# Two attention layers on one core: layer 0's output projection turned round to x1 transposed, by seven block products

## Chip, core and metric

The kernel runs on one core of a Trainium2 chip, in f32 throughout. The metric is device time in microseconds: the median of three runs of the kernel before is 2338.96 us (2338.3 to 2339.53). A profile of one further execution is used for every duration below.

## What is computed

The input x has 8 images of 32 x 32 = 1024 tokens and 256 channels. Layer 0 is attention with four heads, each as wide as all 256 channels, with an output projection, a bias and a residual. Layer 1 is attention with one head whose queries and keys have 32 channels; its values are scaled by gamma and added to its input.

```python
# layer 0
qkv = jnp.einsum('bnc,cd->bnd', xf, W_qkv)              # then split by head into q, k, v
atten = jnp.einsum('bihd,bjhd->bijh', q, k) * scale
atten = jax.nn.softmax(atten, axis=2)
res = jnp.einsum('bijh,bjhd->bihd', atten, v)
res = jnp.einsum('bnd,dc->bnc', res, W_out) + b_out + xf
# layer 1, on res
f, g, h = x@Wf + bf, x@Wg + bg, x@Wh + bh
y = gamma * (jax.nn.softmax(g f^T) @ h) + x
```

## The kernel before, in words

**Folded weights.** For each head, W_q W_k^T and W_v W_out are multiplied once (`fold_weights`, L293), so a head has only a query projection (wqk, C x C), scores against x itself, products of the exponentials with x itself, and an output projection (wvo, C x C). The exponentials are taken without subtracting a maximum; a flag made at the end from the inverse sums (`judge`, L997) chooses whether a general version is run afterwards.

**Seven products.** Query projection, scores and products are 2 x 2 block multiplications in the manner of Strassen and Winograd: seven block products in place of eight. `seven` (L234) returns three tasks. Task one makes products 1 (bank x), 6 (bank y) and 5 (bank z); ScalarE copies x to e, VectorE adds u = y + e. Task two adds product 2 to x and 7 to y; ScalarE copies x out, VectorE makes v = y + e and z + v. Task three adds 4 to y and 3 to z; VectorE adds y + e and z + u. The operands need four sums a side (`sum_a`, `sum_b`, L204 and L214), made by VectorE.

**Order of the work.** A step is a pair (unit, block): a unit is one head of layer 0 of one image (`Layer0`) or layer 1 of one image (`Layer1`), a block is 512 of the 1024 tokens. The units run image by image; layer 1 of image b-1 is put between heads 1 and 2 of image b, and that of image 6 after all heads of image 7. Layer 1 of image 7 (`final`) comes after the loop. PE, VectorE and ScalarE run in exactly the order in which the program issues their instructions (`manual_schedule`, L870); DMA queues on SP and the Pool engine are ordered by the framework. Within a step `put` (L922) gives every task a place between -2 and 11, and the tasks are issued in order of place. In a layer 0 step the score tasks have the places 0, 2, 4, 6, 8 and 10 (two times three tasks of `seven`). Around them lie, of the step before (`one`), the sums over its exponentials (`sums`, L559) with the sums over keys, and tasks one and two of its products; of the step before that (`two`), task three of its products, the inverse of its sums and its projection.

**Sums over keys.** For each block VectorE adds the sums that the products have made anyway: m (L585), then rs (L590, L591). Pool adds over partitions (`partition_all_reduce`, L593, 128 x 512) into rb; SP writes one row of rb to DRAM (L597) and reads it back as columns st (L600); VectorE inverts st (`invert`, L606).

**Projection.** `project` (L629) makes, per block, two tasks of four matmuls: y (128 channels x 128 tokens) is the stationary operand, wvo (128 x 256) the moving one. Rows of tokens come out in one bank po of the pool psm. VectorE multiplies by the inverse sum and adds to the rows of x1 (L648), which `residual` (L425) has filled with x + b_out.

**Layouts.** The scores need x transposed (xT), the products need x by rows. `load_x` loads rows; `turn_rows` (L357) turns rows into xT by DMAs of 32 x 32 squares and transposes on VectorE, a head before they are wanted; layer 1 needs x1 transposed, made in the same way through the fg tile as scratch, and by PE transposes for the last image (L986). `queries_apart` (L687) makes layer 1's f and g: PE, ScalarE into a tile with tag m0 (L698), then 16 SP DMAs (L718, L719), at the places 1.5 to 1.9 of the step before layer 1.

**Buffers.** The tags in L866 to L869 give the number of buffers: rows 4, xT 2, m0, ss, rs and rb 1 each; ps has six PSUM banks and psm two. m and fg2 share m0.

Of the kernel before, what the change touches and what calls it, by code (L numbers as in the profile page):

```python
# [10 lines left out]
F32 = mybir.dt.float32  # L11
# [9 lines left out]
def kernel(  # L21
# [14 lines left out]
):  # L36

# [111 lines left out]
    bout_sb = const.tile([P, C], F32, tag="bout", name="bout_sb")  # L149
    bfg_sb = const.tile([P, 1], F32, tag="bfg", name="bfg_sb")  # L150
# [7 lines left out]
    def load_rest():  # L158
        with nc.allow_non_contiguous_dma(reason="small bias vectors, loaded once"):
            nc.sync.dma_start(bout_sb, b_out.partition_broadcast(P))  # L160
# [20 lines left out]
    wblocks = {}  # L181
# [52 lines left out]
    def seven(name, width, parts, matmuls, outs, tags, copy, after=None):  # L234
# [7 lines left out]
        def bank(k):  # L242
            banks[k] = tile_of("ps", [P, NB], f"ps{k}_{name}")[:, :width]
# [22 lines left out]
        def one():  # L266
            for k, number in (("x", 1), ("y", 6), ("z", 5)):
                bank(k)
                product(k, number, True)
# [21 lines left out]
    NARROW = dict(e="eh", u="uh", v="w")  # L291

    def fold_weights(h):  # L293
# [20 lines left out]
        def multiply(i, what):  # L314
# [13 lines left out]
            if i == 0:  # L328
# [4 lines left out]
                wblocks[h] = b_operands(blocks, sums)  # L333

# [22 lines left out]
    def turn_rows(b, src, dst, layer, scratch=None):  # L357

# [5 lines left out]
        def end():  # L364
            if b not in dst:
                dst[b] = tile_of("xT", [P, CC, N], f"x{layer}T_{b}")
            return dst[b]

        def flat(t):
            return t.rearrange("p u n -> p (u n)").rearrange("p (s q) -> p s q", q=P)  # L370

        def move(a, c=None):
            to, rows_v = flat(end() if scratch is None else scratch()), flat(src[b])
            if c is not None:
                to, rows_v = to[:, ts(c, NT), :], rows_v[:, c::CC, :]
            for q in range(P // Q):
                nc.sync.dma_start(to[ts(q, Q), :, ts(a, Q)], rows_v[ts(a, Q), :, ts(q, Q)])

        def piece(k, c):
            to = end()[:, c, ts(k, NB)]  # L380
            if scratch is None:
                nc.vector.transpose(to, to)
            else:
                squares = scratch()[:, k, :].rearrange("p (t c q) -> p t c q", c=CC, q=P)
                nc.vector.transpose(to.rearrange("p (t q) -> p t q", q=P), squares[:, :, c, :])
# [39 lines left out]
    def residual(b):  # L425


        def piece(i):
            if i == 0:
                rows1[b] = tile_of("rows", [P, NT, C], f"x1_{b}")  # L430
# [702 lines left out]
```

## Time and profile before

| | |
|---|---|
| Median of three runs | 2338.96 us |
| The profiled execution's own time | 2338.61 us |
| Its span, first to last instruction | 2336.7 us |
| Granted TensorE clock | 0.999 |
| PE busy | 2326.9 us in 10394 matmul records |
| VectorE busy | 1481.7 us in 2398 instructions |
| ScalarE busy | 522.5 us in 875 instructions |
| Pool busy | 211.5 us in 79 instructions |
| DMA, mean | 18 GB/s |

The profile is one execution as the hardware profiler took it. A group's row gives line, engine, operation, the tiles written and read, the shapes and the count, then the busy time with the mean of one in ns, then the idle time of the engine just before, with what ended it. A timeline row gives start, duration, engine, line, operation and count. An engine's idle time costs only where it is on the chain that ends last. An f32 matmul shows as two records, and the ends of matmul records are modelled, so starts are the better measure.

### The profile page before, as it was taken

The numbers are of one execution on the slowest core, as the hardware profiler recorded it, in microseconds if no ns is written. First come the engines' busy times: TensorE is split into PE (matmuls) and PEld (weight loads), VectorE is DVE, ScalarE is ACT, GpSimd is POOL, SyncE is SP. The second block draws the span as 40 slices with busy tenths as digits, with TensorE's granted clock in tenths as the row PEclk, the third lists the DMA queues.
The fourth block names the chain that finished last, engine by engine and source line by source line (L and its number), as shares of the span: only waits on it lengthen the run. The fifth ranks groups of instructions, "written<-read, shape, count | busy, mean of one in ns | idle before, by whom it ended". The sixth has DMA issues, their size and how long they took to land.

```text
span 2336.7 us, 26026 instructions
## 1 busy us (share of the span) xinstructions
PE 2326.9 (100%) x10394; PEld 1918.8 (82%) x10394; DVE 1481.7 (63%) x2398; ACT 522.5 (22%) x875; POOL 211.5 (9%) x79
## 2 busy tenths in 40 slices
PE   9999999999999999999999999999999999999999
PEld 7888888788878888788887888878888788888877
DVE  6667775377754767557774577645776457766635
ACT  2222222222221222212222122221222222222222
POOL 0111111011110111101111011110011101101110
PEclk9999999999999999999999999999999999999999
DMA  4000010100101001110011000110001100000100
GB/s 138 1 1 1 1 37 14 34 1 11 27 17 32 1 19 21 19 29 1 19 26 18 24 1 19 30 18 19 1 19 30 19 19 1 1 1 1 30 7 31
DMA packets 170257, 42.94 MB, mean 18 GB/s; under 512 B 158160, under 2 KB 163024, under 8 KB 170128
## 3 DMA queue, kind: packets, MB, share of 16 engines
q1 hardware_dynamic: 170128, 41.20, 8.0%
q8 instruction: 84, 1.38, 0.3%
q14 instruction: 45, 0.37, 0.1%
HBM read 13.37 MB, written 8.52 MB: 9 GB/s over the span
## 4 chain that ended last, share of the span: by engine, by line
PE 99%; DVE 1%; DMA 0%; issue 0%; ACT 0%
PE psy_y L247 14%; PE psy L247 14%; PE psx L247 9%; PE pa_l L834 9%; PE po L637 9%; PE psx_y L247 9%; PE psz_y L247 9%; PE psz L247 9%; PE psy_q L247 4%; PE psx_q L247 2%; PE psz_q L247 2%; PE pr_v_l L466 2%; PE ps_l L746 1%; PE pm_fg L703 1%; PE pwqk L318 0%; PE pwvo L318 0%
## 5 line engine op out<-in xcount | busy, mean ns | idle before, releaser
L593 POOL PARTITION_ALL_REDUCE rb<-rs x64 | 206.9, 3233 | 2046.6 <-DVE rs L591 2019.8
L247 PE MATMUL psx<-q,x0T 128*128 128x256 f32 x1024 | 263.6, 380 | 0.0
L247 PE MATMUL psy<-qs,xs 128*128 128x256 f32 x1024 | 263.0, 379 | 0.0
L247 PE MATMUL psz<-q,xs 128*128 128x256 f32 x1024 | 262.8, 379 | 0.0
L541 ACT ACTIVATE p<-p 128x1024 f32<-128x1024 f32 x128 | 135.3, 1057 | 554.8 <-DVE p L264 554.8
L247 PE MATMUL psy_y<-s,xt 128*128 128x256 f32 x1024 | 242.4, 380 | 0.1
L637 PE MATMUL po<-wvo,y 128*128 128x256 f32 x1024 | 241.9, 379 | 0.0
L247 PE MATMUL psx_y<-p,x 128*128 128x256 f32 x1024 | 241.9, 379 | 0.0
L834 PE MATMUL pa_l<-v_l,s_l 128*128 128x257 f32 x1024 | 232.1, 381 | 0.4 <-DVE v_l L729 0.4
L247 PEld LDWEIGHTS psx<-q,x0T 128*128 128x128 f32 x1024 | 194.0, 190 | 45.2 <-issue 21.0
L637 PEld LDWEIGHTS po<-wvo,y 128*128 128x128 f32 x1024 | 194.6, 190 | 39.5 <-issue 14.8
L834 PEld LDWEIGHTS pa_l<-v_l,s_l 128*128 128x128 f32 x1024 | 193.8, 190 | 36.6 <-issue 10.5
L247 PEld LDWEIGHTS psx_y<-p,x 128*128 128x128 f32 x1024 | 194.7, 190 | 34.0 <-issue 8.6
L247 PEld LDWEIGHTS psy_y<-s,xt 128*128 128x128 f32 x1024 | 191.9, 190 | 30.6 <-issue 2.4
L247 PEld LDWEIGHTS psy<-qs,xs 128*128 128x128 f32 x1024 | 194.5, 190 | 27.0 <-DVE qs L512 0.4
L247 PEld LDWEIGHTS psz<-q,xs 128*128 128x128 f32 x1024 | 194.7, 190 | 26.3
L264 DVE TENSOR_TENSOR u<-psy,e 128x512 f32<-128x512 f32 x128 | 88.4, 691 | 144.3 <-ACT e L270 73.4
L276 ACT ACTIVATE p<-psx 128x512 f32<-128x512 f32 x128 | 76.4, 597 | 413.7 <-PE psx L247 413.6
L264 DVE TENSOR_TENSOR v<-psy,e 128x512 f32<-128x512 f32 x128 | 87.8, 686 | 124.5 <-PE psy L247 124.5
L247 PE MATMUL psy<-qs,x0T 128*128 128x256 f32 x512 | 131.6, 380 | 0.7 <-DVE v L264 0.7
L648 DVE SCALAR_TENSOR_TENSOR x<-po,inverse,x 128x256 f32<-128x256 f32 x256 | 111.9, 478 | 31.3 <-PE po L637 22.4
L270 ACT COPY e<-psx 128x512 f32<-128x512 f32 x128 | 73.8, 576 | 257.8 <-PE psx L247 257.8
(120 smaller groups left out, 2839.8 us busy)
## 6 DMA issues: line engine op xcount, KB each, us to landing
out_dram<-x SPq DMA_DIRECT2D x15, 512.0 KB, 2.6
x<-in_x_dram SPq DMA_DIRECT2D x14, 512.0 KB, 4.6
x0T<-x SPq DMA_DIRECT2D x224, 32.0 KB, 1.9
fg<-x SPq DMA_DIRECT2D x112, 64.0 KB, 2.1
fg<-fg SPq DMA_DIRECT2D x56, 64.0 KB, 2.0
w<-in_L_conv_W_qkv_dram SPq DMA_DIRECT2D x4, 512.0 KB, 7.3
x<-in_x_dram SPq DMA_DIRECT2D x4, 256.0 KB, 4.8
w<-in_L_conv_W_qkv_dram SPq DMA_DIRECT2D x4, 256.0 KB, 6.4
```

The costliest lines, as they stand in the source:

```text
L247: nc.tensor.matmul(banks[k][:, ts(i, w)], lhsT=lhsT, rhs=rhs, start=first and n == 0, stop=True, skip_group_check=True,)
L264: nc.vector.tensor_tensor(dst, shaped(banks[k]), shaped(other), ALU.add)
L270: nc.scalar.copy(scratch("e"), banks["x"])
L276: copy(outs["11"](), shaped(banks["x"]))
L466: nc.tensor.matmul(pm[:, ts(j, C)], lhsT=src()[:, c, ts(2 * t2 + j, P)], rhs=w()[:, c, :], start=(c == 0), stop=(c == CC - 1),)
L541: exp(both, both)
L593: nc.gpsimd.partition_all_reduce(t, r.rearrange("p e i -> p (e i)"), P, bass_isa.ReduceOp.add)
L637: nc.tensor.matmul(pm[:, ts(j, C)], lhsT=self.y[blk][:, c, ts(2 * t2 + j, P)], rhs=folded[self.h][1][:, c, :], start=(c == 0), stop=(c == ...
L648: nc.vector.scalar_tensor_tensor(acc, pm[:, ts(j, C)], inverse[:, n : n + 1], acc, ALU.mult, ALU.add)
L703: nc.tensor.matmul(pm[ts(k, half)], lhsT=w[:, c, :], rhs=x1T_of[b][:, c, ts(k, NB)], start=(c == 0), stop=(c == CC - 1),)
L746: nc.tensor.matmul(pm, lhsT=self.f[ts(r, CK), ts(j0 + r, P)], rhs=self.g[ts(r, CK), ts(blk, NB)], start=True, stop=True,)
L834: nc.tensor.matmul(pm[:, : C + 1], lhsT=p[:, j, ts(ti, P)], rhs=v[:, j, : C + 1], start=(j == 0), stop=(j == NT - 1),)
```

## The change

It turns the projection round. wvo is now the stationary operand, cut into four 128 x 128 blocks with their four sums (`oblocks`), and y the moving one, cut into two halves of 256 tokens a channel half, with four sums a block. `project` becomes a `seven` of three tasks with one matmul per product; its banks y and z share one bank of psm, x takes a bank of ps. The result o comes out transposed, channels by tokens, in a tile with tag m0. It is multiplied by the inverse sums spread over all partitions (rb) and added to x1T by an accumulating DMA that Pool issues. To have the inverse along the free axis, `invert` writes the inverted columns to a row in DRAM and reads it back to all partitions, two more DMAs on SP; in the last step `invert_all` inverts the all-reduced sums directly.

So x1 exists transposed first. `residual` fills x1T from xT on ScalarE with the bias by channel. Layer 1 reads x1T without a turn; its rows are made by `turn_back` with 32 DMAs an image, for the final additions. The last image's PE transposes go, and its fg projection moves behind the loop.

The sums over keys become three additions of 128 x 512, then one of 128 x 256; the product's sums s2 and s4 share a tile, and s3 overwrites the block a21. The query sums are made by block instead of by head. The next image's rows are loaded at head 1 instead of head 2, and the turns follow a step or two earlier than before; rows has 3 buffers, xT has 3. Head 3's weights are loaded into an xT buffer. Places change accordingly.

```diff
-    def seven(name, width, parts, matmuls, outs, tags, copy, after=None):
+    def seven(name, width, parts, matmuls, outs, tags, copy, after=None, two_banks=False):
...
         def bank(k):
-            banks[k] = tile_of("ps", [P, NB], f"ps{k}_{name}")[:, :width]
+            if not two_banks:
+                banks[k] = tile_of("ps", [P, NB], f"ps{k}_{name}")[:, :width]
+            elif k == "z":
+                banks[k] = banks["y z"][:, width : 2 * width]
+            else:
+                t = tile_of("psm", [P, NB], f"ps{k}_{name}")
+                banks["y z"], banks[k] = t, t[:, :width]
...
-                product(k, number, True)
+                product(k, number, k != "z" or not two_banks)
...
+            else:
+                t4 = const.tile([P, 4, P], F32, tag=f"wo{h}", name=f"wo{h}")
+                sums = [t4[:, k, :] for k in range(4)]
+                blocks = [t[:, c, ts(e, P)] for e in range(CC) for c in range(CC)]
+                run(sum_a(sums, *blocks))
+                oblocks[h] = a_operands(blocks, sums)
...
+            if c == 0:
+                x1T_of[b] = tile_of("xT", [P, CC, N], f"x1T_{b}")
+            nc.scalar.activation(
+                x1T_of[b][:, c, :], xT_of[b][:, c, :], AF.Identity, bias=boutT_sb[:, c : c + 1]
             )
...
+                    t = tile_of("qs", [P, 3, HB], f"qs_{self.name}_{blk}")
...
-                sums = [t[:, 1], s2, s3, t[:, 0]]
+                sums = [t[:, 1], t[:, 0], blocks[2], t[:, 0]]
...
+            def add(k):
+                t = made["t"]
+                if k == 1:
+                    made["r"] = tile_of("rs", [P, 2, HB], f"rs_{n}")
+                r = made["r"]
+                tt(r, t[:, :, 0, :] if k == 1 else r, t[:, :, k, :], ALU.add)
...
         def invert(self, blk):
...
+            inv = inverse[:, n : n + HT]
+            nc.vector.reciprocal(inv, self.r[blk])
+            if blk in self.rb:
+                return
+            line = tile_of("line", [1, NB], f"inv_{self.name}_{blk}")
+            with nc.allow_non_contiguous_dma(reason="columns turn into a row"):
+                nc.sync.dma_start(line.rearrange("o (t p) -> p (o t)", p=P), inv)
+            self.rb[blk] = t = tile_of("rb", [P, NB], f"invb_{self.name}_{blk}")
+            nc.sync.dma_start(t, line[0].partition_broadcast(P))
+
+        def invert_all(self, blk):
+
+            self.rb[blk] = t = tile_of("rs", [P, NB], f"invb_{self.name}_{blk}")
+            nc.vector.reciprocal(t, self.total[blk])
...
         def project(self, blk):
...
+                if i == 0:
+                    y = self.y[blk]
+                    t = tile_of("yt", [P, 3, HB], f"yt_{n}")
+                    blocks = [y[:, c, ts(e, HB)] for c in range(CC) for e in range(2)]
+                    sums = [blocks[1]] + [t[:, k] for k in range(3)]
+                    made["l"] = sum_b(sums, *blocks)
+                    made["b"] = b_operands(blocks, sums)
+                made["l"][i]()
+
+            def out(c, e):
+                if "o" not in made:
+                    made["o"] = tile_of("m0", [P, CC, NB], f"o_{n}")
+                return made["o"][:, c, ts(e, HB)].unsqueeze(1)
+
+            def add():
+                o = made["o"]
+                nc.vector.tensor_tensor(
+                    o, o, self.rb[blk].unsqueeze(1).broadcast_to([P, CC, NB]), ALU.mult
+                )
+                nc.gpsimd.dma_start(
+                    x1T_of[self.b][:, :, ts(blk, NB)], o, accum_op=ALU.add
+                )
...
+                lambda number: [(0, oblocks[self.h][number], made["b"][number])],
...
+            put([partial(u.invert, k)], 1.9)
+            ysums, tasks, add = u.project(k)
+            put(ysums, *((1.6, 1.7, 1.8, 3.2) if l0 else (2.6, 2.7, 2.8, 3.1) if blk == 0 else
+                         (1.1, 1.2, 1.3, 2.1)))
+            put(tasks, *((3, 5.5, 7) if l0 else (5.2, 6, 7.2) if blk == 0 else
+                         (3, 5, 7) if nxt else (2.1, 3, 4.5)))
+            put(add, 8.6 if nxt else 5)
...
-            put(sums[:2] + sums[3:], *((2.2, 3.2, 4.2) if l0 else (0.8, 2.2, 4.5)))
-            put(sums[2:3], 5.2 if l0 else 5.5)
-            put(keys, *((6.2, 8.2) if l0 else (7.6, 9.6)))
+            put(sums, *((0.9, 2.2, 4.2, 5.6) if l0 else (0.8, 2.2, 3.5, 5.5)))
+            put(keys, *((6.3, 6.6, 7.6, 8.7) if l0 else (6.3, 7.6, 8.3, 8.7)))
...
+        if l0 and blk == 0:
+            put(a.query_sums(1), 1.3, 2.3, 3.3, 4.3)
...
-        if l0 and a.h == 2 and blk == 0 and a.b + 1 < B:
+        if l0 and a.h == 1 and blk == 0 and a.b + 1 < B:
             load_x(a.b + 1)
...
+                moves, turned1 = turn_back(a.b - 1)
+                put(moves, *range(1, 9))
...
+            put(turned1, 0.6, 2.9, 4.2, 5.1)
         if nxt is None:
-            put(transpose_rows(B - 1, rows1, x1T_of, 1), 2.5, 4.5, 8.1, 8.2)
-            put(final.queries(), 2.4, 6.5, 9)
+            fg = final.queries()
+            moves, turned1 = turn_back(B - 1)
+            put(moves, *[9.1 + 0.1 * k for k in range(8)])
...
-    run(own[:1], s0[:1], prod[:1], p0[:1], s0[1:], prod[1:2], p0[1:2])
-    weave((prod[2:] + own[1:], 0, 1), (s1, 0.3, 0.7), (p1[:2], 0.55, 0.95), (p0[2:], 0.1, 0.9))
+    run(own[:1], prod[:1], fg, s0[:1], p0[:1], prod[1:2], s0[1:], p0[1:2])
+    weave((prod[2:] + own[1:], 0, 1), (s1, 0.3, 0.7), (p1[:2], 0.55, 0.95), (p0[2:], 0.1, 0.9), (turned1, 0.3, 1))
```

## The prediction

> **What bounds the kernel now.** First the page: busy shares and the chain that ended last.
>
> ```profile
> PE 2326.9 (100%) x10394; PEld 1918.8 (82%) x10394; DVE 1481.7 (63%) x2398; ACT 522.5 (22%) x875; POOL 211.5 (9%) x79
> PE 99%; DVE 1%; DMA 0%; issue 0%; ACT 0%
> ```
>
> TensorE is the bound: 2326.9 of 2336.7 us busy, 99% of the chain. A matmul less is time less unless PE starts to wait. Then PE's timeline, for what one matmul costs:
>
> ```profile
> 493.81 1.89 PE L637 MATMUL po<-wvo,y 128*128 128x256 f32 x8
> 495.54 1.03 PE L247 MATMUL psy<-qs,x0T 128*128 128x256 f32 x4
> ```
>
> Start to start, 8 records take 1.73 us. A 128x256 f32 matmul leaves two records (1024 records / 64 blocks = 16 for the 8 matmuls of L637's loops), so one costs **0.432 us**; the row mean of 380 ns counts overlap twice. Then the groups kept apart by shape, for VectorE and Pool:
>
> ```profile
> L593 POOL PARTITION_ALL_REDUCE rb<-rs x64 | 206.9, 3233 | 2046.6 <-DVE rs L591 2019.8 <-DVE y L264 26.8
> L648 DVE SCALAR_TENSOR_TENSOR x<-po,inverse,x 128x256 f32<-128x256 f32 x256 | 111.9, 478 | 31.3 <-PE po L637 22.4
> L580 DVE TENSOR_TENSOR ss<-p 128x1024 f32<-128x1024 f32 x64 | 77.7, 1214 | 0.0
> L585 DVE TENSOR_TENSOR m<-ss 128x1024 f32<-128x1024 f32 x64 | 77.8, 1215 | 0.8 <-DMA fg<-fg 0.7
> L590 DVE TENSOR_TENSOR rs<-m 128x512 f32<-128x512 f32 x64 | 43.5, 680 | 0.0
> L591 DVE TENSOR_TENSOR rs<-rs 128x256 f32<-128x256 f32 x64 | 27.2, 425 | 2.2
> L264 DVE TENSOR_TENSOR y<-psz_y,v_y 128x256 f32<-128x256 f32 x64 | 27.1, 424 | 2.2
> L382 DVE STREAM_TRANSPOSE x0T<-x0T 128x512 f32<-128x512 f32 x28 | 19.6, 701 | 0.0
> ```
>
> The row of m names a DMA as releaser. SP's and VectorE's timelines at that place (image 3, head 1, block 1):
>
> ```profile
> 942.51 0.59 SPq L719 DMA_DIRECT2D fg<-fg  x1
> 944.62 1.22 DVE L585 TENSOR_TENSOR m<-ss 128x1024 f32<-128x1024 f32 x1 [0.19 <-DMA fg<-fg]
> ```
>
> m and layer 1's fg2 (L698) share the one m0 buffer; m waits until the last of the 16 fg moves has landed. Then the windows view of a plain step, head 3's block 0 of image 1 (PE, PEld, DVE, ACT, POOL busy, in that order):
>
> ```profile
> 486.05:513.67 27.62, 27.62 (x129) 24.26 (x128) 22.72 (x37) 6.04 (x10) 4.94 (x2) 1.00 0.01 1
> ```
>
> VectorE is busy 82% of this step and PE has no gap. Last, PE near the end:
>
> ```profile
> 2306.34 3.92 PE L834 MATMUL pa_l<-v_l,s_l 128*128 128x257 f32 x17 [0.39 <-DVE v_l L729]
> ```
>
> At the tail VectorE already sets PE's pace.
>
> **What the skill says.** (1) "VectorE: DVE Perf Modes", The TRN2 errata: an f32 tensor_tensor takes (N+151)/0.96 ns: 424, 691, 1224 for 256, 512, 1024; the rows agree (425, 680, 1214), so halved width doesn't halve the price. (2) "PSUM — Partial Sum Buffer", PSUM bank collisions: two engines on one bank must be ordered, whatever the columns. Before, y and z have banks of their own, so the trace doesn't show it; with both in one, a VectorE read of y also waits for z's matmul. (3) "DMA: Bandwidth & Descriptors", Latency and other measured facts, and Anatomy of one DMA: a Pool-issued DMA costs about 1 us of emission, then about 2.0 us + bytes/436e3; an estimate for 512 KB is 1 + 3.2 us. No Pool DMA is in this trace.
>
> **The change, part by part**, against the profiled execution (2338.61 us: span 2336.7 + 1.9 around it; the runs' median is 2338.96).
>
> *Projection on PE.* 8 matmuls become 7, same shape: 64 x 0.432 = **-27.6 us**. Image 7's 8 transposes by PE go (px 0.49 + 0.43 + 0.87, start to start): **-1.8**. Both are on the path.
>
> *VectorE.* Per block: project was 4 x 0.478 = 1.91; it becomes 4 sums at 0.425, 5 adds at 0.424 and a 128x1024 multiply at 1.21, or 5.03. Keys: 1.215+0.680+0.425 = 2.32 becomes 3 x 0.680 + 0.425 = 2.47. Query sums: 2 x 0.685 becomes 4 x 0.425. Together +3.6 x 64 = +230; the residual's 21 us go to ScalarE (16 x 1.06). VectorE ends near 1,690 us, 73%: room on average, so what counts is order. I laid out one step by hand, block 0 of a head, from the start of its first score task, each instruction after its inputs (about 0.2 us from PE to VectorE, 0.06 back, as the timelines show). Third product task 2.6 to 6.05; score task two to 7.77; then the projection's first task needs t2 at 8.20. VectorE: last y add 6.25, one query sum, ysums 6.9, 7.3, 7.7: t2 ends 8.15. The reciprocal follows at 8.1, v at 8.2 to 8.9; score task three needs v at 9.07. So it fits with 0.05 to 0.15 us to spare. 25 such steps (both predecessors layer 0); bound 0 to 0.5 each, I take 0.04: **+1.0**. In block 1 the next queries' task gives 2.6 us more cover: nothing, and 0.4 each if backlog ate it. The same layout holds the other edits of a step: sum one moves ahead of the third product task into the idle before the y adds; sum four overwrites s2 and so waits for product y6, read by PE at 14.2, when VectorE arrives at 17.8; s3 in place of a21 waits for nothing younger. The value sums (block 1 of head 0) and turns keep 2 to 3 us of idle ahead of the product's tasks. 0 for all of these; half a microsecond a step if that idle is gone.
>
> *PSUM banks.* The projection's x takes one of the six ps banks from its first task to its second, beside three of the score and three of the product. The product's y and z need banks at 12.5 and 14.3; the score's x is free at 7.8, the last product's two at 5 and 6.7. No wait, so 0; at most 0.3 a step if a later bank is drawn (not in the sum). psm needs one bank a block instead of two.
>
> *Sums to columns and back.* The last key add moves to 8.7, behind the multiply and its Pool DMA. By the layout it ends 1.2 us before the step's end; DMA emission 1, all-reduce 3.23, then line and st as now (3.3 us from all-reduce to landing): st lands 6.0 us into the next step, needed at 8.1. Cost 0, cover 2.1 us; past it each us stops VectorE's queue, with v behind it, and PE. The new row and broadcast (SP, two DMAs, some 5 us) end by 14; the multiply comes at 23. Hidden.
>
> *fg moves against o.* The new o tile takes m0's single buffer. In the step of queries_apart (7 times) the clock from the score task's start (923.28 in image 3) is: pm_fg ends 8.0, fg moves landed 21.3 (944.6 above); invert now puts two more DMAs on SP, up to 1.2 later. The projection's second task runs 17.9 to 18.8 on PE, and its copy and add into o want m0 at 18.7, not at 21.3 as m did. ScalarE and VectorE stop there; the third task wants that bank's read at 21.4, and gets it at 21.3 + 0.5 to 22.5 + 0.5. Bound 0 to 2.5 per image, I take 1.2: 7 x 1.2 = **+8.4**.
>
> *Layer 1, block 0.* Tasks one and two of the projection are adjacent (5.2, 6): y7 needs u, which waits for z5, a value add (0.75) and a transpose (0.70). Bound 0 to 0.6, I take 0.3 x 7 = **+2.1**.
>
> *Next image a head sooner; turn_back; residual.* The two 512 KB x loads issue on SP at the start of head 1; the rows buffer they take was last read a step earlier, so SP, with st behind them, isn't held (0.8 us of issue). Their 32 turn moves (SP, 21 us) go beside layer 1's second block, where VectorE is light and only invert's two DMAs and an output store share the queue; the transposes follow in head 2's first block, which has no projection, and the key sums a step later. The residual on ScalarE (2 x 1.06 an image, ScalarE is 22% busy) delays an exp by at most 1 us, with its reader a step away. turn_back issues 32 SP DMAs of 32 KB where turn_rows issued 16 of 64 KB: about 0.65 us each (median 609 ns at L377), 21 us of a 27 us step; st may lose up to 1 us there, within its cover. 0.
>
> *Start.* Four small sums enter head 0's fold ahead of the key sums (about 1.2), half-size query sums return 1.0: bound -1 to +2, I take **+0.3**.
>
> *End.* fg now comes after the loop, straight ahead of the first scores (+0.4 for its copies). Its x1T waits for the last accumulate: 10.4 us of PE lie over 2.3 (adds, multiply) + 4.2 (estimate): covered. turn_back's 32 moves then need 21 us, and four transposes (2.8 us) enter VectorE's queue ahead of the v adds that already held PE 0.39. I take 0.4 + 3.8 = **+4.2**, bounds 0 and 7. The 512-wide reciprocal has no row; 0.7 to 4.5 us, in a light step: 0.
>
> Sum: -27.6 -1.8 +1.0 +8.4 +2.1 +0.3 +4.2 = **-13.4**: 2338.6 - 13.4 = **2325.2 us**, taken against the median too.
>
> **Rivals.** *The covers hold* (24%): m0 frees in time, the tail's transposes slip into gaps; only about 2 us is lost of 29.4: 2311. For it: the step shown already held 22.7 us of VectorE work with no PE gap. Against it: m's wait in the trace.
>
> *Slower, by the sums' way round* (17%): Pool's queue. If issuing the accumulate takes Pool over 3.1 us rather than 1, st comes after VectorE asks for it in the 25 block-0 steps. Slower than before needs 13.4 + 4.7 us more, 0.72 us a step, an issue of 3.8 us; at 4.5 us, 25 x 1.4 = 35: 2360. For it: all-reduce alone holds Pool 3.23 us, and no row prices a Pool DMA. Against it: the skill's 1 us.
>
> *The stalls eat the gain* (14%): each at its upper bound (m0 17, layer 1 4, tail 7, start 2): -29.4 + 30 gives 2339. For it: these bounds share a cause, VectorE's fuller queue. Against it: they lie in different steps, and ScalarE's 22% leaves it quick to resume.
>
> **Numbers.** The forecast case has 45%, its own range 2318 to 2333. About 0.2% (4.7 us) is what a measurement can tell from no change. Faster: 43 of the 45, the 24: 0.67; same: the 14 and 2: 0.16; slower 0.17. The range runs from the low edge of the covered case, 2309, to where the slow case begins, 2343.
>
> **What would show it.** Right: seven 128x256 matmuls a block with PE gapless in plain steps; a ScalarE or VectorE wait on an fg move in the projection of queries_apart's step, with a PE gap of about 1 us; a later v_l wait at the tail. Wrong: PE waiting on VectorE in every block-0 step, reciprocals waiting for st, Pool DMA issues over 3 us, or no gap at fg.

## The result, and the profile after

The changed kernel takes 2476.03 us (median of 4 runs, 2474.34 to 2479.75) against 2339.07 us before: ratio **1.0588**, 95% interval 1.057 to 1.0606. The forecast was 2325.2 us, so the sign is wrong: 137 us are lost where 13 were to be won. The profiled execution took 2476.43 us, with a span of 2474.6 us; its differences are taken against the 2336.7 us of before.

First the page of the changed kernel, busy shares and the chain that ended last:

```profile
PE 2334.2 (94%) x10250; PEld 1903.4 (77%) x10250; DVE 1645.2 (66%) x2963; ACT 585.4 (24%) x1015; POOL 288.6 (12%) x143
PE 86%; DVE 6%; DMA 4%; SPq 2%; issue 1%; ACT 0%; DVEq 0%; ACTq 0%
```

TensorE has 144 records less, as the change says, but it is no longer busy all the time: its share of the chain falls from 99% to 86%, and VectorE, DMAs and SP's queue come into it. None of them is a bound by volume (VectorE is busy 1645 us, where the prediction had near 1,690). So the time is in waits. The waits view for PE of the changed kernel (who waited for whom: total, times, longest) names them:

```profile
PE psy_o L257 <- DVE o L274: 64.4, 7, 10.9
PE psy_o L257 <- DVE yt L691: 37.9, 26, 2.7
PE psy_q L257 <- DVE y L274: 15.9, 18, 0.9
PE psy L257 <- DVE v L274: 5.5, 5, 2.0
PE pa_l L897 <- DVE v_l L792: 3.3, 1, 3.3
```

There are two large groups: 7 waits of some 9 us, one in each step that makes layer 1's f and g, and 26 + 18 small ones, in most steps of layer 0. The trace of before had no PE wait over 1.4 us. To see how much each kind of step lost, waits that the view doesn't list included, I took the starts of task one of every product (psx_y) from PE's timelines and compared the stretches between neighbours. "Forecast" is the prediction's own terms, laid on the same stretches (0.432 us saved a projection); the last column is the best kernel of the experiments below.

| Stretch of PE's timeline | before, us each | after, us each | after minus before, in all | forecast | last kernel minus before |
|---|---|---|---|---|---|
| 25 with a plain block-0 step's projection | 16.40 | 17.65 | +31.2 | -9.8 | -6.3 |
| 18 with a plain block-1 step's projection | 22.41 | 23.10 | +12.4 | -7.8 | -3.0 |
| 7 before the queries_apart gap | 18.47 | 18.0 to 20.8 | +3.6 | -3.0 | -3.0 |
| 7 with the queries_apart gap | 11.22 | 22.0 to 24.0 | +82.5 | +8.4 | +0.3 |
| around layer 1 (26 stretches) | | | -0.2 | -3.9 | +0.5 |
| 44 others | 11.22 (one 14.9) | the same | 0.0 | 0.0 | 0.0 |
| start | | | -0.5 | +0.3 | -0.7 |
| end, after the last such start | 93.1 | 101.9 | +8.9 | +2.4 | +0.3 |
| sum | | | +137.9 | -13.4 | -11.8 |

**The small waits.** Here is the plain step that the prediction showed for before, head 3's block 0 of image 1, in the windows view of the changed kernel: 28.87 us where it was 27.62, with VectorE's busy time down, not up.

```profile
507.59:536.46 28.87, 27.46 (x127) 23.87 (x126) 21.13 (x39) 6.78 (x12) 3.52 (x3) 1.00 0.07 11
```

VectorE's and PE's timelines of the changed kernel in that step, in brackets the idle time ahead of the instruction and what ended it:

```profile
513.83 1.23 DVE L613 TENSOR_TENSOR ss<-p 128x1024 f32<-128x1024 f32 x1 [3.41 <-PE psz_y L257]
514.97 0.42 DVE L274 TENSOR_TENSOR y<-psy_y,e_y 128x256 f32<-128x256 f32 x1
...
516.88 0.42 DVE L691 TENSOR_TENSOR yt<-y 128x256 f32<-128x256 f32 x1
...
517.36 0.70 PE L257 MATMUL psy_o<-yt,wo 128*128 128x256 f32 x2 [1.41 <-DVE yt L691]
```

The instruction to look at is the first of the four sums over the exponentials (`sums`), the prediction's "sum one"; most of the expectations below call it the first key sum. It stands idle for 3.41 us, for a matmul of the product's third task. It writes a new tile ss, ss has one buffer, and the third product task is the last reader of the old one. The y adds, which could have run during that task, stand behind it in VectorE's fixed order; with them the sums of y come late, and the projection's second task with those. In all, `ss` waits 164.9 us in 50 steps:

```profile
L613 DVE TENSOR_TENSOR ss<-p 128x1024 f32<-128x1024 f32 x64 | 78.1, 1220 | 164.9 <-PE psz_y L257 164.9
```

**The large waits.** The DMA issues of the changed kernel (KB each, median us from issue to landing):

```profile
x1T<-o POOLq DMA_DIRECT2D x64, 512.0 KB, 5.0
invb<-inv SPq DMA_DIRECT2D x63, 256.0 KB, 4.8
...
st<-line SPq DMA_DIRECT2D x64, 2.0 KB, 2.1
inv<-inverse SPq DMA_DIRECT2D x63, 2.0 KB, 8.8
fg<-fg SPq DMA_DIRECT2D x56, 16.0 KB, 8.7
```

The row of inverses, 2 KB, takes **8.8 us**; the way back of the same shape, a row turned into columns (st), takes 2.1. And the timelines in image 2's step of queries_apart show who stands behind that row:

```profile
680.41 0.52 SPq L647 DMA_DIRECT2D inv<-inverse  x1
...
682.43 0.58 SPq L781 DMA_DIRECT2D fg<-fg  x1
...
688.93 0.34 SPq L649 DMA_DIRECT2D invb<-inv  x1
689.32 0.51 SPq L782 DMA_DIRECT2D fg<-fg  x1
...
694.24 0.42 DVE L274 TENSOR_TENSOR o<-psy_o,v_o 128x256 f32<-128x256 f32 x1 [10.49 <-DMA fg<-fg]
694.72 1.22 PE L257 MATMUL psy_o<-yt,wvo 128*128 128x256 f32 x2 [8.84 <-DVE o L274]
...
696.59 1.83 PE L257 MATMUL psx<-q,x0T 128*128 128x256 f32 x4
698.25 1.03 PE L257 MATMUL psy<-qs,xs 128*128 128x256 f32 x4
```

The broadcast (invb) must wait for the row; SP's queue is in order, so the sixteenth fg move, issued behind the broadcast, waits too: from 682.4 to 689.3. It lands at about 694, and o, which shares m0 with the tile that the moves read, is written then. TensorE stands for 8.84 us.

**The clock.** After this gap the matmuls run at half speed for some 3.5 us: the four psx take 1.83 us above, the four psy behind them 1.03 as ever. In the windows view of the changed kernel the column before the last two is the granted clock; the rows are the stretch before the gap, the gap, the 3.8 us behind it, and the rest:

```profile
675.00:686.00 11.00, 10.63 (x48) 9.04 (x48) 5.86 (x10) 1.83 (x3) 0.00 (x0) 1.00 0.24 47
686.00:694.70 8.70, 0.00 (x0) 0.00 (x0) 0.46 (x2) 0.57 (x2) 0.00 (x0) 0.61 0.17 38
694.70:698.50 3.80, 3.78 (x10) 3.06 (x11) 3.77 (x7) 0.34 (x2) 0.00 (x0) 0.54 0.02 4
698.50:709.00 10.50, 10.50 (x53) 8.36 (x51) 7.03 (x13) 2.50 (x5) 4.43 (x2) 1.00 0.29 50
```

That is what the Trainium skill says, "TensorE: Matmul & The Clock Gate", What's actually happening: half clock after an idle window of about 3.4 us, full clock again after a busy one. The trace agrees with half clock and with about 3.5 us of it behind this gap, of which half is lost. Over the 6 us behind each of the seven gaps the clock was 0.54 to 0.73, 0.63 on average, which makes 15 us lost in all. In one point the trace differs from the page: half clock stands behind shorter gaps too, such as one of 2.04 us in this kernel (0.72 over the 6 us from 980.11).

### The profile page after: what moved, and what is told of

Same layout as the page of the kernel before. It is cut to its first block, busy times and chain, and to the rows that moved or that the text cites. A ratio compares the mean times of both kernels' runs of the same rounds, so it can differ in the third digit from the quotient of the medians.

```text
span 2474.6 us, 27238 instructions
## 1 busy us (share of the span) xinstructions
PE 2334.2 (94%) x10250; PEld 1903.4 (77%) x10250; DVE 1645.2 (66%) x2963; ACT 585.4 (24%) x1015; POOL 288.6 (12%) x143
## 3 DMA queue, kind: packets, MB, share of 16 engines
q1 hardware_dynamic: 223232, 58.91, 11.8%
## 4 chain that ended last, share of the span: by engine, by line
PE 86%; DVE 6%; DMA 4%; SPq 2%; issue 1%; ACT 0%; DVEq 0%; ACTq 0%
PE psy_y L257 13%; PE psy L257 12%; PE psx_y L257 9%; PE psz L257 8%; PE psz_y L257 8%; PE pa_l L897 8%; PE psx L257 8%; PE psy_o L257 6%; PE psy_q L257 3%; DMA inv<-inverse 3%; PE psz_q L257 2%; DVE ss L613 2%; PE pr_v_l L495 2%; PE psx_q L257 2%; PE psx_o L257 1%; PE ps_l L809 1%
## 5 line engine op out<-in xcount | busy, mean ns | idle before, releaser
L703 POOL DMA_DIRECT2D x1T<-o x64 | 78.0, 1219 | 1759.2 <-issue 518.4
L626 POOL PARTITION_ALL_REDUCE rb<-rs x64 | 231.6, 3620 | 358.9 <-DVE rs L624 358.9
L257 PE MATMUL psx<-q,x0T 128*128 128x256 f32 x1024 | 269.5, 387 | 0.0
L257 PE MATMUL psy_y<-p,xt 128*128 128x256 f32 x1024 | 241.9, 379 | 0.0
L257 PEld LDWEIGHTS psy_y<-p,xt 128*128 128x128 f32 x1024 | 194.7, 190 | 26.3
L613 DVE TENSOR_TENSOR ss<-p 128x1024 f32<-128x1024 f32 x64 | 78.1, 1220 | 164.9 <-PE psz_y L257 164.9
L257 PE MATMUL psy_y<-ss,xt 128*128 128x256 f32 x512 | 121.0, 379 | 0.0
L257 PE MATMUL psz_y<-ss,xt 128*128 128x256 f32 x512 | 121.0, 379 | 0.0
L257 PE MATMUL psz_y<-ss,x 128*128 128x256 f32 x512 | 121.0, 379 | 0.0
```

Source lines behind the costliest of these rows:

```text
L257: nc.tensor.matmul(banks[k][:, ts(i, w)], lhsT=lhsT, rhs=rhs, start=first and n == 0, stop=True, skip_group_check=True,)
L613: made["l"][i]()
L626: nc.gpsimd.partition_all_reduce(t, r.rearrange("p e i -> p (e i)"), P, bass_isa.ReduceOp.add)
L703: nc.gpsimd.dma_start(x1T_of[self.b][:, :, ts(blk, NB)], o, accum_op=ALU.add)
```

## The experiments

The first theory was: **(A)** two separate orders of the change cost the time, sum one's place and the queue on SP ahead of o. Rivals: **(B)** the cost is in the turned projection itself (its banks, its adds, Pool's DMA), and these edits only move it; **(C)** the clock is the larger part. In the kernels that write the row in another order (first in experiment 5), lines from L654 on stand 1 higher than in the changed kernel, and lines from L700 on 8 higher.

**1. Another buffer for fg2.**

```diff
-                made["t"] = t = tile_of("m0", [P, NB], f"fg2_{b}")
+                made["t"] = t = tile_of("qs", [P, NB], f"fg2_{b}")
```

> The changed kernel, with layer 1's fg2 in a tile of tag qs instead of m0, so that o no longer waits for the fg moves. Theory A (o waits for the shared m0 buffer until SP has issued the last fg move behind its wait for the inverse row; PE then stands 9 us and afterwards runs at half clock): the 64.4 us of PE waits before psy_o go, and 7 x 10.24 us at half clock, worth 7 x 5.1 = 36 us, with them; 2476 - 100 = 2376 us. Rival B (VectorE has become too full, and m0 only names where it shows): PE waits for VectorE elsewhere instead, less than 30 us gained, above 2446 us.

Measured: 2434.05 us (2428.47 to 2436.24), ratio to before 1.0403 (1.0386 to 1.042): 42 us better than the changed kernel, between the two expectations. The waits of this kernel's PE:

```profile
PE psy_o L257 <- DVE yt L691: 38.0, 26, 2.7
PE psy_y L257 <- DVE v_y L274: 21.6, 7, 3.7
```

o's wait is gone, and a new one stands in its place: the multiply now waits for the broadcast, 4.8 us in image 2, and PE for what is behind it on VectorE. So the shared m0 was only where the late row hit first.

**2. Sum one behind the third product task.**

```diff
-            put(sums, *((0.9, 2.2, 4.2, 5.6) if l0 else (0.8, 2.2, 3.5, 5.5)))
+            put(sums, *((2.1, 2.2, 4.2, 5.6) if l0 else (0.8, 2.2, 3.5, 5.5)))
```

> The changed kernel, with sum one of a layer 0 step at place 2.1 instead of 0.9, so that VectorE passes the y adds and the projection's sums before it meets the wait for the single ss buffer. Theory A: PE's waits for yt (37.9 us), for y before the query projection (16.0) and for v (5.5) go; 2476 - 59 = 2417 us. Rival B (VectorE's work is too long for the step): the same 1.2 us is only moved behind, and PE waits for v or u by as much; 2455 us or more.

Measured: 2423.41 us (2420.15 to 2425.78), ratio 1.036 (1.0343 to 1.0377): 53 us better, A's figure to within 7 us. PE's waits of this kernel:

```profile
PE psy_o L257 <- DVE o L274: 44.0, 7, 6.8
PE psy L257 <- DVE v L274: 18.2, 10, 3.8
...
PE psy_o L257 <- DVE yt L691: 2.7, 1, 2.7
```

25 of the 26 waits for yt are gone, and with them the 18 of the queries' task for y (8 short ones for v_q, 3.7 us in all, are new). That half of A holds: sum one's place made the small waits. The 53 us are a net gain: the waits for v, which A expected to go, grew from 5.5 to 18.2 us, and the seven large waits stay, 44.0 us instead of 64.4. A second buffer for ss, which would test the reason by itself, was not tried.

**3. The fg moves ahead of the row in SP's queue.**

```diff
-                put(moves, 1.6, 1.7, 1.8, 1.9)
+                put(moves, 1.55, 1.56, 1.57, 1.58)
```

> The changed kernel, with the four fg move tasks at places 1.55 to 1.58 instead of 1.6 to 1.9: the same buffer is shared, but all 16 moves stand ahead of the inverse's two DMAs on SP. Theory A (the last move is held by SP's wait for the inverse row, 8.5 us): it is issued some 7 us earlier, the wait of o falls to under 1.5 us each and no half clock follows; 2376 to 2390 us. Rival C (the fg moves themselves land late, since accumulates and turn moves fill the DMA engines): the wait stays over 6 us each; above 2446 us.

Measured: 2463.58 us (2460.75 to 2467.54), ratio 1.0538 (1.052 to 1.0555): only 12 us better. The timelines of this kernel in the same step:

```profile
683.18 1.33 SPq L647 DMA_DIRECT2D inv<-inverse  x1
692.80 0.33 SPq L649 DMA_DIRECT2D invb<-inv  x1
...
697.83 1.23 DVE L700 TENSOR_TENSOR o<-o,invb 128x1024 f32<-128x1024 f32 x1 [6.19 <-DMA invb<-inv]
```

The order in the queue did what was expected of it, o hardly waits now, but the row goes out behind 16 moves, lands 9.6 us later, and the multiply is late instead. Whoever stands first, the other pays the row. A had to be put more sharply: not the queue, but the 8.8 us of the row.

**4. Matmuls to keep the clock up.** Twenty matmuls of which nobody reads the result, at place 6.9 of the seven steps.

```diff
+                def warm(x=xT_of[a.b]):
+                    pm = tile_of("psm", [P, NB], f"warm_{a.b}")
+                    for _ in range(20):
+                        nc.tensor.matmul(pm[:, :HB], lhsT=ident, rhs=x[:, 0, :HB], start=True, stop=True)
+
+                put([warm], 6.9)
```

> The changed kernel, with 20 matmuls of 128x256 (8.6 us, into a spare bank that nobody reads) put ahead of the projection's third task in the seven steps of queries_apart, where PE waits 9.2 us anyway. Theory A (the idle stretch itself makes the clock fall to half for 10.24 us): the seven half clock stretches go, and the matmuls fit into the wait; 2476 - 36 = 2440 us. Rival D (the clock falls for another cause): the stretches stay, 2476 us or a little more.

Measured: 2550.47 us (2546.03 to 2551.91), ratio 1.0901 (1.0882 to 1.0919). Inconclusive: the added matmuls draw a bank that the late o still holds (67.7 us of waiting in 7 times), so they ran behind the gap and not in it, and paid for themselves. Nothing follows for the clock. My expectation of 36 us for the clock was too much as well: more than half of the seven stretches of 10.24 us at half clock lay in the gaps, where TensorE stood anyway, and what was lost behind them is 15 us.

**5. The row written in another order.** A partition holds four neighbouring inverses (16 bytes). The changed kernel writes them 512 bytes apart, so that the row comes out in order; here they go out as they lie, and the multiply reads the broadcast through a view that turns the order back.

```diff
-                nc.sync.dma_start(line.rearrange("o (t p) -> p (o t)", p=P), inv)
+                nc.sync.dma_start(line.rearrange("o (p t) -> p (o t)", p=P), inv)
...
+                    o4 = o.rearrange("q c (t p) -> q c t p", p=P)
+                    r4 = self.rb[blk].rearrange("q (p t) -> q t p", p=P)
+                    nc.vector.tensor_tensor(
+                        o4, o4, r4.unsqueeze(1).broadcast_to([P, CC, HT, P]), ALU.mult
+                    )
```

> The changed kernel with one edit: the row of inverses goes to DRAM in the order in which a partition holds it (four neighbouring elements, 16 bytes, instead of four single elements 512 bytes apart), and the multiply reads the broadcast row through a view that turns the order back. Theory A (the 8.8 us that this row takes is a matter of its 512 single elements of 4 bytes; SP stands behind it, so that the last move of f and g, and o after it, come late): the row lands in some 2 to 3 us, SP is free again before the move, o's 64.4 us of TensorE wait fall below 10, the half-clock stretches of that step go with the gap (12 to 14 us), the waits for yt (37.9) and for y's bank (15.9) stay: about 2400, 2390 to 2412. Theory D (the landing is the queue's and not the elements'[...]): the row still takes over 7 us and the time stays above 2460.

Measured: 2412.62 us (2411.93 to 2415.39), ratio 1.0319 (1.0301 to 1.0336): 63 us better, just past the upper edge of A's range. The packets and the row's landing in this kernel, and its largest PE waits:

```profile
DMA packets 216588, 94.29 MB, mean 39 GB/s; under 512 B 180032, under 2 KB 184896, under 8 KB 216448
...
inv<-inverse SPq DMA_DIRECT2D x63, 2.0 KB, 1.6
```

```profile
PE psy_o L257 <- DVE yt L692: 38.8, 26, 3.5
PE psy_q L257 <- DVE y L274: 15.9, 18, 0.9
PE psy_o L257 <- DVE o L274: 14.9, 7, 2.9
```

Same bytes, same queue, same place: 1.6 us instead of 8.8, so D is out. The packets of the changed kernel are

```profile
DMA packets 240780, 94.29 MB, mean 38 GB/s; under 512 B 204224, under 2 KB 209088, under 8 KB 240640
```

and the difference, 24192, is 63 rows x (512 - 128): one packet per element against one per partition. The Trainium skill has the rule, "DMA: Bandwidth & Descriptors", Rules for kernel authors: a last dimension that isn't contiguous is lowered to one descriptor per element. The trace agrees, and adds the price. o still makes TensorE wait, 14.9 us where A had under 10: 2.1 us an image, 2.9 at most. That is the wait which the prediction described, with its bound of 2.5.

**6, 7, 8. The edits together.** The row and sum one; the buffer of fg2 and sum one; all three.

> Both causes taken away together: the row of inverses in neighbouring elements, and the first key sum at place 2.1 instead of 0.9. Theory A (two separate causes: the row's landing, worth some 76 us, and the sum's wait for the single buffer ss, worth 53): they add, about 2347, 2335 to 2360, and what is left over the kernel before is some 8 us: layer 1's first block, the end, and small waits in layer 0's steps. Theory F (the turned projection has a further cost that these two hide, such as the Pool queue or the all-reduce's tail): above 2375, with a new wait of over 30 us on TensorE.

> The first two edits together, with the row of inverses as in the changed kernel: the second tile of f and g in another tag than o's, and the first key sum at place 2.1. Theory A (the row's late landing still makes the multiply late even where o doesn't wait for the moves): gains add, 2476 - 42 - 53 = 2381, and TensorE still waits some 21 us for v_y in the seven steps with queries. Theory G (the half clock of the gap that the two share goes as well): below 2370.

> All three edits: the row of inverses in neighbouring elements, the second tile of f and g in another tag than o's, the first key sum at place 2.1. If what a step loses is only these three, TensorE's waits in layer 0's blocks fall to a few us and the saving of 29.4 us on TensorE is seen, less 4.0 at layer 1's first block, 3.3 at the end and some 5 of small waits: 2322 to 2335, below the kernel before. If the other tag brings a wait of its own (it also holds the score tiles' sums), or the plain steps' row too still comes late, 2340 to 2365.

Measured: row and sum 2348.52 us (2347.29 to 2349.57), ratio 1.0038 (1.0024 to 1.0053); buffer and sum 2343.92 us (2339.91 to 2346.65), 1.002 (1.0013 to 1.0026); all three 2339.93 us (2338.06 to 2342.35), 1.0004 (0.9995 to 1.0013). The first is where A had it, though not by A's sum: alone the two brought 63 + 53 = 116 us, together 128. The second is far from adding up: 42 + 53 = 95 us were expected to come back, and 132 did. That lies in G's range, but G's reason is too small, since all the half clock behind the seven gaps is worth 15 us. The timelines of that kernel in image 2's step show more:

```profile
643.14 0.36 SPq L647 DMA_DIRECT2D inv<-inverse  x1
...
651.33 0.51 SPq L782 DMA_DIRECT2D fg<-fg  x1
...
658.78 1.23 DVE L700 TENSOR_TENSOR o<-o,invb 128x1024 f32<-128x1024 f32 x1 [0.36 <-DMA invb<-inv]
```

Counted from the start of the fg projection in that step, the row goes out at 4.4 us instead of 11.4: with the sum at its later place the row stands ahead of the sixteen moves in SP's order, and no longer behind twelve of them. It still takes over 8 us, but the multiply then waits 0.36 us. So the two causes are not separate, as A had them: sum one's place also decided when the row started (in experiment 2's kernel, too, the row stands ahead of the moves). With fg2 in its own buffer, a slow row is hidden if it starts early.

All three together are no faster than the kernel before, and the forecast for them was 2322 to 2335. The stretches show two places: the plain steps win 0.1 to 0.2 us on average instead of 0.43, and the end loses 11.6 us. PE's timeline at the end of the kernel with all three:

```profile
2254.95 1.22 PE L257 MATMUL psy_o<-yt,wo 128*128 128x256 f32 x2 [3.49 <-DVE yt L692]
...
2258.63 4.86 PE L905 MATMUL pa_l<-v_l,s_l 128*128 128x257 f32 x16
...
2306.66 28.16 PE L905 MATMUL pa_l<-v_l,s_l 128*128 128x257 f32 x116 [3.21 <-DVE v_l L800]
```

Two gaps, and slow matmuls behind each: 4.86 us for what else takes 3.63 to 3.73, and 28.16 for what took 25.37 before. The first gap is the 512-wide reciprocal of `invert_all`, 3.35 us, ahead of yt's sums on VectorE; the second holds the last image's four transposes (0.70 each), ahead of the last v add.

**9. The end mended.** The reciprocal behind the projection's second task, the transposes into the stretch of the last products.

```diff
-                put([partial(u.invert_all, k)], 0.6)
-            put([partial(u.invert, k)], 1.9)
+                put([partial(u.invert_all, k)], 3.2)
+            put([partial(u.invert, k)], 1.9 if nxt else 3.3)
...
-    weave((prod[2:] + own[1:], 0, 1), (s1, 0.3, 0.7), (p1[:2], 0.55, 0.95), (p0[2:], 0.1, 0.9), (turned1, 0.3, 1))
-    weave((final.products(0), 0, 1), (p1[2:], 0, 0.9), ([judge, decide], 0.9, 1))
+    weave((prod[2:] + own[1:], 0, 1), (s1, 0.3, 0.7), (p1[:2], 0.55, 0.95), (p0[2:], 0.1, 0.9))
+    weave((final.products(0), 0, 1), (turned1, -0.2, 0.9), (p1[2:], 0, 0.9), ([judge, decide], 0.9, 1))
```

> The three edits together and the last block's order mended: the 512-wide reciprocal goes behind the projection's second task (it stood ahead of yt's sums on VectorE, 3.35 us), the last image's four transposes go out of the stretch with the v adds into the one after it. Theory A (the end loses 11.6 us against the kernel before by two TensorE gaps, 3.5 for yt and 3.2 for v_l, each followed by a stretch at half clock, 2.4 and 2.8 us): both gaps and both stretches go: 2340 - 11 = 2329, 2325 to 2333, faster than the kernel before. Theory H (VectorE is full there, so that the work that is moved stands in the way at its new place): a new gap of over 2 us, 2334 to 2342.

Measured: 2331.38 us (2330.65 to 2332.31), ratio 0.9967 (0.9955 to 0.998). Both gaps are 0.4 us now, and the end is within 0.2 us of the kernel before. Theory A. (Ahead of the reciprocal VectorE had also waited 3.8 us for Pool's sum; the mended kernel waits 3.9 us at that place for layer 1's matmuls, so that wait is not what was lost.)

**10. Layer 1's projection tasks apart.** On top of the mended end:

```diff
-            put(tasks, *((3, 5.5, 7) if l0 else (5.2, 6, 7.2) if blk == 0 else
+            put(tasks, *((3, 5.5, 7) if l0 else (5.2, 7.1, 8.1) if blk == 0 else
```

> As the kernel with the mended end, and layer 1's first block puts its three projection tasks apart (5.2, 7.1, 8.1 instead of 5.2, 6, 7.2), so that other matmuls stand between the first and the second. Theory A (the adjacent tasks wait 0.15 us for u_o and 0.4 us for the bank that a v_l add reads, 0.57 us an image of 7): some 1 to 4 us less than without it, 2326. Theory H (the third task's add comes nearer to the end of the step and the multiply after it later): no gain, within 2 us of the kernel with the mended end or above it.

Measured: 2332.72 us (2332.12 to 2333.11), ratio 0.9973 (0.9962 to 0.9983). No gain: the waits for u_o (1.1 us in 7) are no longer among this kernel's largest, the 2.9 us for the bank that a v add reads are unchanged, and the time is no better. Theory H; left out again.

**11. One gap by itself.** In the kernel before, VectorE is held up ahead of the last v add by work that nobody reads.

```diff
+    def pause():
+        t = tile_of("rs", [P, NB], "pause")
+        nc.vector.memset(t, 1.0)
+        for _ in range(3):
+            nc.vector.reciprocal(t, t)
+
+    own.insert(-1, pause)
```

> A control on the kernel before, not on the changed one: a memset and three 512-wide reciprocals on a tile of ones that nobody else reads are put on VectorE ahead of the last v add of the end, so that TensorE has one gap of some 10 us there and nothing else is changed. If a gap costs only itself: 2339 + 10 = 2349, and the 116 matmuls behind it take 25.4 us as before. If the clock that is granted falls to half for about as long as the gap was (Theory C, as the gaps of the changed kernel seemed to show): the matmuls behind it take some 30 us and the time is 2353 to 2355.

Measured: 2354.26 us (2352.71 to 2355.09), ratio 1.0064 (1.005 to 1.0078). The matmuls behind the gap, in the kernel before and then with the pause:

```profile
2306.34 25.37 PE L834 MATMUL pa_l<-v_l,s_l 128*128 128x257 f32 x116 [0.39 <-DVE v_l L729]
...
2319.34 27.52 PE L834 MATMUL pa_l<-v_l,s_l 128*128 128x257 f32 x116 [13.30 <-DVE v_l L729]
```

The gap is 12.9 us longer than before (other VectorE work fell behind the pause too, which I hadn't counted), and the 116 matmuls take 2.15 us more than their 25.37; the time grew by 15.0 = 12.9 + 2.1. The time lies in Theory C's range only because the gap came out longer than planned; the matmuls take 27.5 us and not 30. So a gap does cost more than itself, in the kernel before as well, but some 2 us and not half of the gap: a gap of 13.3 us costs 2.15 behind it, and one of 3.2 us (all three edits, above) costs 2.8. The cost doesn't grow with the gap.

**12. A query sum behind v and p.** On top of the mended end, for the 0.2 us that a plain block-0 step still lost:

```diff
-            put(a.query_sums(1), 1.3, 2.3, 3.3, 4.3)
+            put(a.query_sums(1), 2.05, 2.3, 3.3, 4.3)
```

> The kernel with the mended end, and in block 0 of each head one query sum (0.33 us on VectorE) goes behind the score's v and p instead of ahead of the sums of y. Theory A (in the 25 plain block-0 steps the three yt sums end 0.04 us before the projection's second task reads them, and TensorE loses 0.1 us at each of two tasks there without showing a gap): 0.1 to 0.2 us a step comes back, 2331 - 3 to 5 = 2327, 2325 to 2329. Theory J (the small loss comes from the bank in which the projection's y and z follow each other, not from the sums): no change, 2330 to 2333.

Measured: **2327.62 us** (2327.25 to 2328.59), ratio to before 0.9953 (0.9939 to 0.9966). Theory A. The projection's tasks in head 3's block 0 of image 1 now follow each other every 0.43 us:

```profile
490.35 0.59 PE L257 MATMUL psx_o<-y,wvo 128*128 128x256 f32 x2
490.78 0.59 PE L257 MATMUL psy_o<-yt,wo 128*128 128x256 f32 x2
491.21 0.59 PE L257 MATMUL psy_o<-y,wo 128*128 128x256 f32 x2
491.64 1.03 PE L257 MATMUL psy<-qs,x0T 128*128 128x256 f32 x4
```

With the sum in front they stood at 491.26, 491.80, 492.34 and 492.77, the second and the third each 0.1 us late. No idle time was shown for them: only the starts tell it. This is the fastest kernel of the study, 11 us under the kernel before. With it rival B falls: the same turned projection wins once the work around it stands in another order. Of C there remains the half clock behind the changed kernel's gaps: 15 us behind the seven large ones and some 5 behind three others (2.04, 2.69 and 3.27 us), of 137.

## Why the prediction was wrong, point by point

**PE, -27.6 and -1.8: right as prices.** 144 records less, 0.43 us from start to start for each pair of matmuls. The saving is there, under the waits.

**"Sum one moves ahead of the third product task into the idle before the y adds ... 0 for all of these": wrong, and the first of the two steps that failed.** The sum does go into that idle time, but it can't run in it: it takes the only buffer of ss, which the third product task still reads, so it turns idle time ahead of the y adds into a wait in front of them. In the layout I asked of every instruction when its inputs were ready, not when its output's buffer was free (for sum four I did ask, and found its reader). Taking it away brought back 53 us alone (experiment 2), 64 on top of the quick row and 90 on top of fg2's own buffer. I had named "PE waiting on VectorE in every block-0 step" as a sign that I was wrong, and it is what the profile shows.

**The t2 margin, +1.0: mechanism right, size too small.** "0.05 to 0.15 us to spare" was the right place. With sum one out of the way a plain block-0 step still lost 0.2 us on its three close projection products, 25 x 0.2 = 5; one 0.33 us sum moved out of the way brought back 3.8 us (experiment 12).

**fg moves against o, +8.4: mechanism right, its size wrong by ten, and the second step that failed.** o did wait for the last fg move in the seven steps. But "invert now puts two more DMAs on SP, up to 1.2 later" counted what the two cost SP to issue. The second of them waits for the first to land, and SP stands while it does. "The new row and broadcast (SP, two DMAs, some 5 us)" took 8.8 for the row and 4.8 for the broadcast. I had taken the row for the mirror of st's 2.1 us; it isn't: its elements lie apart on the side that is written, and written side by side they landed in 1.6 us (experiment 5). With the row quick the wait is 14.9 us in all, nearer to the 8.4 forecast; with it slow these stretches lost 82.5, 64.4 of it in the listed wait. What is left, 18 us in seven steps, is mostly the 15 us of half clock that I hadn't reckoned with at all; that part is read from the trace and experiment 11, not undone by itself.

**Layer 1 block 0, +2.1:** the two waits of these tasks sum to 2.9 + 1.1 = 4.0 us. The one for u, 0.15 a time, is what I described; the larger, 0.4 a time, is for a bank that a v add reads, and that I had not seen. Spreading the tasks out didn't help.

**End, +4.2:** +8.9 measured, where with the 1.8 of PE transposes that go 2.4 was forecast. The four transposes ahead of v cost about what was forecast (the wait for v_l went from 0.39 to 3.27 us). What I put at 0, "the 512-wide reciprocal ... in a light step", stands ahead of yt: a gap of 2.7 us there; and both gaps have slow matmuls behind them.

**Sums to columns, cover 2.1 us, turn_back and Pool:** the issue of the accumulating DMA took Pool 1.22 us for the estimated 1, all-reduce 3.62 us instead of 3.23. In plain steps st is in time. The rival that ended slower had this as its mechanism, and it was not this: VectorE waits for st only 21.2 us in 12 times. Six of these lie behind turn moves, and TensorE doesn't wait there. The other six lie in the steps with the fg projection, and behind four of them TensorE waits 4.8 us for v. In image 2 the all-reduce ends at 665.9, but SP issues the row of sums only at 671.0, behind turn_back's moves, which had themselves stood some 6 us behind the slow row of inverses. So "st may lose up to 1 us there, within its cover", at 0, was too small. In experiment 12's kernel st is still 0.7 to 1.2 us late in seven steps, with turn_back's moves between its two DMAs, and TensorE waits 2.6 us.

**The rest at nothing:** the next image's turn moves, the loads a head earlier, the residual on ScalarE, the PSUM banks of y and z: no TensorE wait of theirs over a microsecond shows.

So the forecast of 2325 was of a kernel that exists, experiment 12's at 2327.6, but not the one that was to be judged. Even there the agreement is in part luck: the plain steps won 9.3 us where 17.6 were forecast, and the fg moves cost 0.3 where 8.4 were.

## What to carry to other kernels

On an engine with a fixed order, ask of each instruction that is moved earlier two things: are its inputs ready, and has the last reader of the buffer that it writes gone by; if not, everything behind it waits, however idle the engine was. Price a chain of DMAs on one queue by landings, not by issues, and look at both sides' layout: count the pieces that lie in one run, since 2 KB in single elements took over five times as long as the same 2 KB in runs of 16 bytes. And a TensorE gap of 3 us or more cost some 1.5 to 3 us more than itself in these kernels.

## What the runs showed of the hardware that was not expected

- A row of 512 f32 from SBUF (4 a partition) to DRAM: 8.8 us from issue to landing as single elements, 1.6 us as 16-byte runs; from DRAM to SBUF the same single elements took 2.1 us. With the row in front, in the kernel with another buffer and the later sum, seven moves were issued behind it and the eighth only 8.2 us after the row (643.14 and 651.33); the waits view of SP's queue lists such a move as waiting for the row, which it doesn't read (26.6 us in 7 times). Why it waits was not tried.
- A VectorE reciprocal of 128 x 512 takes 3.35 us, where an addition of that size takes 0.68; of 128 x 4, 0.17 us.
- The 128 x 1024 multiply takes 1.22 us, and 2.02 us when one operand is read with a stride of 16 bytes (the view that turns the order back). It costs 50 us of VectorE time in all (63 times 0.8); how much of it lies on the path was not tried.
- A gap's half clock: none behind gaps of up to 1.97 us. Between 2 and 3 us it came and stayed away: in experiment 5's kernel the 6 us behind a gap of 2.48 had a clock of 0.72 (from 677.38), and those behind one of 2.90 had 1.00 (from 382.25). Every gap of 3 us or more had it, with 2.8 us lost behind one of 3.2 and 2.15 us behind one of 13.3.
- Pool takes 1.22 us to issue the 512 KB accumulating DMA, which lands 5.0 us after the issue starts; 1 + 3.2 had been estimated.
